# A decoder kernel on one Trainium2 core: the second composed weight by seven block products, with its sums of blocks on GpSimd, and the first weight weighed on ScalarE

## The chip, the cores and the metric

The kernel runs on one core of a Trainium2 chip. The metric is the device time of one execution in microseconds (us); lower is better. A core has five engines that run side by side and wait for each other by semaphores: TensorE (PE in the profile, its weight loads PEld) multiplies matrices into the accumulation memory PSUM, VectorE (DVE) and ScalarE (ACT) work elementwise and can read PSUM, GpSimd (POOL) works elementwise on SBUF only and issues the gathers here, and SyncE (SP) issues transfers.

## The reference, cut to what matters

The input x is 8 sequences of 256 tokens with 256 features, in float32. Three stages follow each other, each closed by x = layernorm(x + stage(x)):

1. four layers of self-attention (four local heads, four causal linear heads) and a two-layer perceptron of width 1024,
2. a cross-attention to a context,
3. a perceptron whose two weights are themselves composed:

```
vals, idx = top_k(logits, 32)
w = softmax(vals)
W = einsum('k,kir,kro->io', w, A[idx], B[idx])      # r = 64
# first weight:  A (64, 256, 64),  B (64, 64, 1024) -> W1 (256, 1024)
# second weight: A (64, 1024, 64), B (64, 64, 256)  -> W2 (1024, 256)
h = gelu(x @ W1);  y = h @ W2
```

The change is about composing W1 and W2. With the 32 chosen primitives stacked along r, each is a matrix product with an inner size of 32 x 64 = 2048. Neither depends on x, so the kernel composes them while the attention layers run.

## The kernel before

**Slots.** The main loop at line 1173 runs over slots s = 1 to 32 (four layers by eight sequences). In a slot several units at different stages interleave: `new` is the attention of unit s (projections, scores, exponentials), `old` that of unit s-1 (values and output projection), `after` that of unit s+1 (its moments, normalising and transposing), and `ff` the perceptron of unit s-4, which exists from s = 4 on. All engines but SyncE follow program order (`manual_schedule`, line 1101), so the order of calls in the loop is the order of each engine's queue. While the weights are being composed, `filled` is true (line 1177). A loop of 16 more slots from line 1283 does cross-attention and the composed perceptron.

**The composing.** It is split into 16 groups (line 321): eight for the first weight (n=0), eight for the second (n=1). A group has PG = 2 inner chunks of 128, that is two pairs of primitives. It passes four steps:

- `gather` (Group.__init__, line 325): GpSimd issues indirect transfers that fetch the rows of A (tiles `ga`) and of B (tiles `gbt`, of 128 x 1024 for n=0 and of 128 x 256 for n=1). It runs two groups ahead.
- `weigh` (line 341): A times its softmax weight, four VectorE instructions a group (L350), into `aw`.
- `turns` (line 359): TensorE transposes `aw` (L369) through PSUM banks, and VectorE and ScalarE copy the result to `at`. With at[k] as the stationary operand, this is A transposed, chunk k.
- `block` (line 382): four blocks of 128 x 512. For n=1 each block is two output rows j of 128 x 256, each accumulated over the two chunks k: 4 x 2 x 2 = 16 matmuls of 256 columns a group (L410). VectorE then copies the block to w2c (first group) or adds it to w2c (L420, L422). For n=0 w2c serves as the accumulator, and the last group writes w1c (L400).

`Compose.run` (line 448) does the blocks of the turned group, gathers one more group, and transposes the next. It is called three times in slot 1, twice in slots 2 and 3, and once, near the end of a slot, from slot 4 on. So the first weight is done in slot 4, and the second weight's eight groups are multiplied in slots 5 to 12. Before the loop, slot 0 (lines 1142 to 1167) weighs and transposes the first group.

**Seven products in the perceptron.** `Seven` (line 482) multiplies a matrix of two by two blocks with seven block products in place of eight (a scheme of Strassen's kind). Its products are `one` (line 509, L512: four matmuls of 128 columns each). The sums of blocks of the weights come once a layer from `first_sums` (L476 to L479), those of the tokens once a slot from `turn_sums` (L490 to L493), both on GpSimd.

**GpSimd's queue in a slot with `ff`.** In order: the power of `after.moments()` (L189), `ff.turn_sums()`, the memset of 64 columns of oT in `old.values()` (L801), two bias sums of `after.centre()` (L230), the power of `nxt_m.moments()`, the gathers of `compose.run()` (L302), two bias sums of `nxt_m.centre()`.

**TensorE's order in such a slot.** `new.qkv` (L602, L622), `old.linear_sums`, `old.turn_p` (L767), `ff.turn`, `new.scores` (L653), `old.values` (L784, L797), then `ff.p16` (products 1 and 6), `old.out(0)` (L240, which reads oT), `ff.p5`, `ff.p27`, `old.out(1)`, `ff.p34`, `ff.second(1)` (L561), `after.turn` (L213), `compose.run` (L410, L369), `ff.second(0)`.

**PSUM.** There are two pools of four banks each. Composing, `ff`, `turn` and `out` share `bank_g`; `second(1)` takes a bank there (ps_p_m) that `second(0)` fills up at the end of the slot.

Of the kernel before, what the change touches and what calls it, by code (L numbers as in the profile page):

```python
# [8 lines left out]
F32 = mybir.dt.float32  # L9
I32 = mybir.dt.int32  # L10
AF = mybir.ActivationFunctionType
ALU = mybir.AluOpType
# [3 lines left out]
P = 128  # L16
# [5 lines left out]
def tile_decoder_postln(  # L22
# [29 lines left out]
    nc = tc.nc  # L52

    B, T, D = x.shape
    DEPTH = Wq.shape[0]
    WT = T // P
    NC = D // P
    FF = W1.shape[2]
    NF = FF // P
    HL = 4  # L60
# [8 lines left out]
    NP, _, R = fc1_A.shape  # L69
    TOPK = 32  # L70
    NPAIR = TOPK // 2
# [30 lines left out]
    at = 0  # L102
    offs = {}
    for name, v in (("g1", ln1_g), ("b1", ln1_b), ("g2", ln2_g), ("b2", ln2_b), ("ff", b1)):
        n = v.shape[0] * v.shape[1] // P
# [17 lines left out]
    w1c = const.tile([P, NC, FF], F32, name="w1c")  # L123
    w2c = const.tile([P, NF, D], F32, name="w2c")
# [46 lines left out]
    def bank_g(name):  # L171
        return ps_g.tile([P, 512], F32, tag="bank_g", name=name)
# [78 lines left out]
    comp_stack = ExitStack()  # L251
    comp = comp_stack.enter_context(tc.tile_pool(name="comp", bufs=1))
# [59 lines left out]
    PG = 2  # L312
# [11 lines left out]
    class Group:  # L324
# [16 lines left out]
        def weigh(self):  # L341

            n, g, n_c = self.n, self.g, tables[self.n][2]
            wts = tops[n][2]
            self.aw = []
            for k, a in enumerate(self.a):
                t = g * PG + k
                aw = comp.tile([P, n_c, 2, R], F32, tag="aw", name=f"aw{n}_{t}", bufs=2)
                for e in range(2):
                    nc.vector.tensor_scalar(  # L350
                        aw[:, :, e, :],
                        a[:, e, :].rearrange("p (c r) -> p c r", c=n_c),
                        wts[:, 2 * t + e : 2 * t + e + 1],
                        None,
                        ALU.mult,
                    )
                self.aw.append(aw.rearrange("p c e r -> p c (e r)"))

        def turns(self):
            n, n_c = self.n, tables[self.n][2]  # L360
            self.at = []
            for k, aw in enumerate(self.aw):
                name = f"{n}_{self.g}_{k}"
                at_ = comp.tile([P, n_c * P], F32, tag="at", name=f"at{name}", bufs=4)
                for q in range(0, n_c, 4):
                    ps = bank_g(f"ps_at{name}_{q}")
                    m = min(4, n_c)
                    for c in range(m):
                        nc.tensor.transpose(ps[:, c * P : (c + 1) * P], aw[:, q + c, :], ident)  # L369
                    if n == 0:  # L370
                        copy = nc.scalar.copy if k else nc.vector.tensor_copy
                        copy(
                            at_.rearrange("q (p c) -> q c p", c=NC),
                            ps[:, : m * P].rearrange("q (c p) -> q c p", c=NC),
                        )
                    elif q == 0:
                        nc.vector.tensor_copy(at_[:, :512], ps)
                    else:
                        nc.scalar.copy(at_[:, 512:], ps)
                self.at.append(at_)  # L380

        def block(self, i):
            ps = bank_g(f"ps_w{self.n}_{self.g}_{i}")
            if self.n == 0:
                m, n = divmod(i, 2)
                for k in range(PG):
                    nc.tensor.matmul(  # L387
                        ps,
                        self.at[k][:, m * P : (m + 1) * P],
                        self.b[k][:, n * 512 : (n + 1) * 512],  # L390
                        start=k == 0,
                        stop=k == PG - 1,
                    )

                dst = w2c.rearrange("p f d -> p (f d)").rearrange("p (m o) -> p m o", m=NC)
                dst = dst[:, m, n * 512 : (n + 1) * 512]
                src = ps
                if self.g == NPAIR // PG - 1:
                    final = w1c[:, m, :].rearrange("q (j p) -> q p j", j=NF)
                    nc.vector.tensor_add(  # L400
                        final[:, n * 64 : (n + 1) * 64, :],
                        dst.rearrange("q (p j) -> q p j", j=NF),
                        src.rearrange("q (p j) -> q p j", j=NF),
                    )
                    return
            else:
                for e in range(2):
                    j = 2 * i + e
                    for k in range(PG):
                        nc.tensor.matmul(  # L410
                            ps[:, e * D : (e + 1) * D],
                            self.at[k][:, j * P : (j + 1) * P],
                            self.b[k],
                            start=k == 0,
                            stop=k == PG - 1,
                        )
                dst = w2c[:, 2 * i : 2 * i + 2, :].rearrange("p j d -> p (j d)")
                src = ps
            if self.g == 0:
                nc.vector.tensor_copy(dst, src)  # L420
            else:
                nc.vector.tensor_add(dst, dst, src)  # L422

    class Compose:

# [17 lines left out]
        def turn(self):  # L443
            self.turned, self.weighed = self.weighed, None
            if self.turned:
                self.turned.turns()

        def run(self):
            if self.turned is None:
                return  # L450
            if not self.weighed:
                self.weigh()
            for i in range(4):
                self.turned.block(i)
            self.gather()
            self.turn()

# [24 lines left out]
    class Seven:  # L482
# [26 lines left out]
        def one(self, n, ps, start=False, stop=False):  # L509

            for f in range(4):
                nc.tensor.matmul(  # L512
                    ps[:, f * P : (f + 1) * P],
                    self.ws[n][:, f * P : (f + 1) * P],
                    self.rhs[n],
                    start=start and f == 0,
                    stop=stop and f == 3,
                    skip_group_check=True,
                )
# [50 lines left out]
    class Attention:  # L570
# [99 lines left out]
        def exps(self):  # L670
            name = self.name
            nc.scalar.activation(self.qs, self.qs, AF.Exp)
            nc.scalar.activation(self.ke, self.ke, AF.Exp)
            self.p = []

            self.psum = small.tile([P, HL, 3], F32, tag="psum", name=f"psum_{name}")
            self.head_exps(range(2))

        def head_exps(self, heads):
            for h in heads:  # L680
# [211 lines left out]
    class Context:  # L892
# [29 lines left out]
        def take(self):  # L922
            b0, ps = self.b0, self.ps
            nc.vector.tensor_copy(
                self.cT[:, :, b0 : b0 + 2, :],
                ps[:, : 2 * NC * S2].rearrange("p (c b j) -> p c b j", c=NC, b=2),
            )
# [184 lines left out]
    compose = Compose()  # L1112
    cross = None
    cx = None
    new = Attention(0)
    first = {n: top_k(n) for n in range(2)}
# [43 lines left out]
    compose.gather()  # L1160
    new.scores()
    new.exps()
    new.head_exps((2, 3))
    new.softmax_q()
    new.totals()
    new.divide(range(HL))
# [1 line left out]
    old, new = new, after  # L1168
# [4 lines left out]
    for s in range(1, UNITS + 1):  # L1173
# [3 lines left out]
        filled = cross is None  # L1177
        if after and filled:
            after.moments()
        if new:  # L1180
            new.qkv(nxt_c)
        nxt_c = None
        if s == 1:
            compose.run()
        if s == 2:
# [5 lines left out]
        if ff:  # L1191
            ff.turn()
            ff.turn_sums()
        if new:
            new.scores()
        else:
            cx.sums()
# [35 lines left out]
        if turn_cx:  # L1233
            i = 2 * (s - (UNITS - B + LAG))
            cx.turn(i)
            cx.take()
        if new:
            new.exps()
        if ff:
            ff.second(1)  # L1240
        if after:
            after.turn()
        if new:
            new.head_exps((2, 3))
            new.softmax_q()
        if filled:
            compose.run()
# [6 lines left out]
            nxt_m.centre()  # L1254
        if ff:
            ff.second(0)
        if compose.done() and cross is None:
            comp_stack.close()
            cross = ctx.enter_context(tc.tile_pool(name="cross", bufs=1))
        l, b = divmod(s + 1, B)  # L1260
        if b == B - 2 and l + 1 < DEPTH:
            attn_ws[l + 1] = load_attn(l + 1, nc.scalar)
        l, b = divmod(s + 1 - LAG, B)
# [15 lines left out]
        old, new = new, after  # L1279
# [3 lines left out]
    for s in range(2 * B):  # L1283
        x, ff = nxt_x, nxt_m
        nxt_x = Cross(s + 1, cx) if s + 1 < B else None
        u = UNITS - LAG + s + 2
# [102 lines left out]
```

## Time and profile before

| | us |
|---|---|
| median of 3 runs (lowest to highest) | 1247.95 (1246.93 to 1251.23) |
| the profiled execution | 1256.8 |
| its span, first to last instruction | 1254.9 |
| TensorE busy | 1222.0 (97%) |
| weight loads busy (beside the matmuls) | 969.1 (77%) |
| VectorE busy | 847.8 (68%) |
| ScalarE busy | 628.7 (50%) |
| GpSimd busy | 382.7 (31%) |
| the second weight's matmuls, L410 | 56.6 (256 records) |
| the first weight's matmuls, L387 | 57.4 (128 records) |

Durations below come from the profiled execution. A line of a timeline reads: start, duration, engine, source line, operation, output <- inputs, and in brackets the idle time of the engine ahead of it and what ended it. A group of instructions reads: line, engine, operation, shapes and count, then busy time and mean ns of one, then idle time before. A float32 matmul leaves two records of matmul and two of weight load; matmuls overlap at their ends, so their pace is read from start to start. L12 is line 12 of the kernel.

### The profile page before, as it was taken

The page shows a single profiled execution, that of the slowest core. Times are in us where ns is not written, and L with a number is a line of the kernel's source. Part 1 is how long each engine was busy: PE and PEld are TensorE (multiplying, and loading weights), DVE is VectorE, ACT ScalarE, POOL GpSimd, SP SyncE. Part 2 cuts the span into 40 slices and gives each one's busy share as a digit, 9 for nine tenths or more (in the row PEclk, how much of TensorE's full clock was granted, in tenths as well). Part 3 has the DMA queues.
Part 4 walks back from the last instruction along what each step waited for, and adds up shares of the span by engine and source line. Part 5 has one row for each costly group of instructions (what it writes and reads, how often), then busy time and mean ns, then how long its engine had stood idle before and what let it go on. Part 6 is the DMA issues. An engine that isn't in the chain of part 4 may idle for free.

```text
span 1254.9 us, 23452 instructions
## 1 busy us (share of the span) xinstructions
PE 1222.0 (97%) x8905; PEld 969.1 (77%) x8905; DVE 847.8 (68%) x2435; ACT 628.7 (50%) x1738; POOL 382.7 (31%) x596
## 2 busy tenths in 40 slices
PE   5999999999999999999999999999999999999998
PEld 3555678888888888888878888788888777777787
DVE  5787877767767667777777776777765454556543
ACT  2222544555555556667766677566773334233322
POOL 5445433333334111222322221242213323222210
PEclk8998999999999999999999999999999999999999
DMA  4532212111120021002001000120000000000000
GB/s 131 168 91 83 81 51 81 43 43 43 65 73 20 1 84 39 2 2 72 1 1 39 2 1 17 57 69 1 26 10 10 9 9 9 18 17 9 9 14 22
DMA packets 29502, 47.77 MB, mean 38 GB/s; under 512 B 3150, under 2 KB 22734, under 8 KB 29134
## 3 DMA queue, kind: packets, MB, share of 16 engines
q0 software_dynamic: 6656, 20.98, 5.6%
q10 hardware_dynamic: 13024, 14.07, 3.4%
q1 hardware_dynamic: 9710, 11.23, 2.8%
q8 instruction: 70, 1.15, 0.4%
q14 instruction: 42, 0.34, 0.1%
HBM read 44.17 MB, written 2.10 MB: 37 GB/s over the span
## 4 chain that ended last, share of the span: by engine, by line
PE 92%; DVE 3%; ACT 2%; POOL 1%; issue 1%; another core or an unknown queue 0%; DMA 0%; POOLq 0%; ACTq 0%; DVEq 0%
PE ps_p_m L561 17%; PE qkv_a L622 8%; PE ps_h_m_u L512 7%; PE ps_h_m_a L512 5%; PE ps_w L387 4%; PE ps_w L410 4%; PE ps_h_m_d L512 4%; PE ps_p_a L240 4%; PE ps_qk_a L602 4%; PE ps_p_f L561 4%; PE ps_pT_a L767 3%; PE sc_a L653 3%; PE ps_y_c L1085 2%; PE ps_xq_c L996 2%; PE ps_xk_c L996 2%; PE ps_xv_c L996 2%
## 5 line engine op out<-in xcount | busy, mean ns | idle before, releaser
L561 PE MATMUL ps_p_m<-w,h_m 128*128 128x256 f32 x1024 | 231.5, 379 | 0.0
L561 PEld LDWEIGHTS ps_p_m<-w,h_m 128*128 128x128 f32 x1024 | 189.8, 190 | 23.5 <-ACT h_m L827 0.3
L622 PE MATMUL qkv_a<-wa,xT_a 128*128 128x512 f32 x256 | 115.7, 595 | 0.0
L230 POOL TENSOR_TENSOR x<-x,b 128x256 f32<-128x256 f32 x64 | 48.2, 773 | 209.5 <-DVE xn_m L195 209.4
L685 ACT ACTIVATE p_a<-sc_a,nm_a 128x128 f32<-128x128 f32 (+1 forms) x256 | 103.9, 426 | 1.9 <-DVE nm_a L666 1.7
L622 PEld LDWEIGHTS qkv_a<-wa,xT_a 128*128 128x128 f32 x256 | 49.1, 192 | 48.1 <-issue 46.3
L230 POOL TENSOR_TENSOR x<-x,bo 128x256 f32<-128x256 f32 x64 | 48.2, 772 | 118.4 <-DVE xn_a L195 113.6
L666 DVE TENSOR_REDUCE nm_a<-sc_a 128x1 f32<-128x128 f32 (+1 forms) x256 | 79.7, 353 | 4.4
L827 ACT ACTIVATE h_m<-h_m,cols 128x128 f32<-128x128 f32 x256 | 78.6, 405 | 6.2 <-DVE h_m L549 5.5
L512 PE MATMUL ps_h_m_a<-xT_m,w 128*128 128x128 f32 x512 | 71.4, 283 | 0.0
L302 POOL DMA_INDIRECT ga<-in_L_ffn_fc_A_dram,idx_a x64 | 62.1, 971 | 21.2 <-issue 16.6
L512 PE MATMUL ps_h_m_u<-tx_m,w 128*128 128x128 f32 x512 | 67.6, 275 | 0.0
L629 ACT COPY v<-qkv_a 128x256 f32<-128x256 f32 x64 | 23.8, 372 | 86.3 <-PE qkv_a L622 85.0
L602 PE MATMUL ps_qk_a<-xT_a,wa 128*128 128x256 f32 x256 | 64.0, 395 | 2.8 <-DVE nm_a L666 2.1
L512 PEld LDWEIGHTS ps_h_m_a<-xT_m,w 128*128 128x128 f32 x512 | 63.2, 194 | 4.2 <-issue 1.6
L240 PE MATMUL ps_p_a<-wo,oT_a 128*128 128x256 f32 x256 | 65.4, 380 | 0.0
L662 DVE TENSOR_TENSOR sc_a<-sc_a,causal 128x256 f32<-128x256 f32 x128 | 54.5, 425 | 15.5 <-PE sc_a L653 15.5
L715 DVE TENSOR_TENSOR p_a<-p_a,psum_a 128x384 f32<-128x384 f32 x128 | 62.9, 553 | 1.1
L512 PEld LDWEIGHTS ps_h_m_u<-tx_m,w 128*128 128x128 f32 x512 | 62.3, 192 | 0.0
L602 PEld LDWEIGHTS ps_qk_a<-xT_a,wa 128*128 128x128 f32 x256 | 50.4, 199 | 11.1 <-ACT p_a L685 2.8
L561 PE MATMUL ps_p_f<-w2c,h_f 128*128 128x256 f32 x256 | 57.8, 379 | 0.0
L767 PE MATMUL ps_pT_a<-ident,p_a 128*128 128x128 f32 x384 | 52.3, 278 | 5.6 <-ACT pT_a L772 5.0
(245 smaller groups left out, 2655.2 us busy)
## 6 DMA issues: line engine op xcount, KB each, us to landing
w<-in_L_attn_W_dram ACTq DMA_DIRECT2D x8, 1024.0 KB, 7.6
xwkv<-in_L_xattn_Wkv_dram SPq DMA_DIRECT2D x1, 2048.0 KB
x_c<-in_x_dram SPq DMA_DIRECT2D x8, 256.0 KB, 2.7
out_dram<-y_f SPq DMA_DIRECT2D x16, 128.0 KB, 1.7
x<-in_x_dram ACTq DMA_DIRECT2D x6, 256.0 KB, 2.7
ga<-in_L_ffn_fc_A_dram,idx_a POOLq DMA_INDIRECT x64
xwq<-in_L_xattn_Wq_dram SPq DMA_DIRECT2D x1, 1024.0 KB
xwo<-in_L_xattn_Wout_dram SPq DMA_DIRECT2D x1, 1024.0 KB
```

What stands on the lines that cost most here:

```text
L230: nc.gpsimd.tensor_add(xb[:, i, :], xb[:, i, :], bias)
L240: nc.tensor.matmul(ps[:, i * D : (i + 1) * D], lhs(c, i), w[:, c, :], start=c == 0, stop=c == n_in - 1,)
L512: nc.tensor.matmul(ps[:, f * P : (f + 1) * P], self.ws[n][:, f * P : (f + 1) * P], self.rhs[n], start=start and f == 0, stop=stop and f == ...
L561: nc.tensor.matmul(self.ps[:, i * D : (i + 1) * D], self.h[k][:, f, :], self.w2[:, half * 4 + f, :], start=k in (11, 22) and f == 0, stop= ...
L602: nc.tensor.matmul(ps[:, s * T : (s + 1) * T], wa[:, c, s * HW : (s + 1) * HW], xT[:, c, :], start=c == 0, stop=c == NC - 1,)
L622: nc.tensor.matmul(t, xT[:, c, w * P : (w + 1) * P], wa[:, c, 2 * HW :], start=c == 0, stop=c == NC - 1,)
L666: nc.vector.tensor_reduce(self.nmax[:, h, w : w + 1], sc[:, s], AX.X, ALU.max, negate=True)
L685: nc.scalar.activation(flat[:, s], sc[:, s], AF.Exp, bias=self.nmax[:, h, w : w + 1], accum_out=self.psum[:, h, w : w + 1],)
L715: nc.vector.tensor_tensor(p, p, self.psum[:, h, :, None].to_broadcast([P, 3, P]), ALU.mult)
L767: nc.tensor.transpose(pp[:, k * P : (k + 1) * P], p[:, k, :], ident)
L827: nc.scalar.activation(dst[:, f, :], src[:, f * P : (f + 1) * P], AF.Gelu, bias=col("ff", i))
L996: nc.tensor.matmul(ps[:S2], lhs(c), w[:, c, off : off + 512], start=c == 0, stop=c == NC - 1)
```

## The change

- **Second weight by seven products.** `block` keeps only the first weight's case. For n=1, `seven` computes the group's product, a matrix of 2 x 2 blocks (each 512 x 128, inner size 128) by seven block products of four matmuls of 128 columns: 28 matmuls a group. They accumulate in banks p6, p12, p53 and p74; VectorE takes from these in seven instructions of 128 x 512, into the four quarters of w2c and into `u`, a common sum that all groups share.
- **Sums of blocks.** `combine(0)`, called after `new.qkv` at the top of the next slot, forms four sums of 128 x 128 of B and two of 128 x 512 of A on GpSimd; `combine(1)`, called after `ff.turn_sums`, two more of 128 x 512 of A. Two of the eight are written in place.
- **`final`** adds `u` to three quarters of w2c: three GpSimd sums of 128 x 512, at the top of slot 13. The composing pool is closed there, not at the end of slot 12, and so slot 13 still counts as `filled`.
- **First weight weighed on ScalarE**: `weigh` for n=0 issues `nc.scalar.mul`; for n=1 it stays on VectorE.
- **Exponentials.** `exps` no longer calls `head_exps(range(2))`. In filled slots all four heads' exponentials follow `after.turn()`; in others two come before `ff.second(1)`, as they did.
- **`at`** has two buffers instead of four.

The diff, cut to its core:

```diff
@@ weigh
-                    nc.vector.tensor_scalar(
-                        aw[:, :, e, :],
...
+                    if n == 0:
+                        nc.scalar.mul(dst, src, w)
+                    else:
+                        nc.vector.tensor_scalar(dst, src, w, None, ALU.mult)
@@ turns
-                at_ = comp.tile([P, n_c * P], F32, tag="at", name=f"at{name}", bufs=4)
+                at_ = comp.tile([P, n_c * P], F32, tag="at", name=f"at{name}", bufs=2)
@@ block
-            else:
-                for e in range(2):
-                    j = 2 * i + e
-                    for k in range(PG):
-                        nc.tensor.matmul(
-                            ps[:, e * D : (e + 1) * D],
-                            self.at[k][:, j * P : (j + 1) * P],
-                            self.b[k],
...
+        def combine(self, part):
+            if part:
+                a, s2, s4 = self.rest
+                nc.gpsimd.tensor_sub(s4, a[0][1], s2)
+                nc.gpsimd.tensor_sub(a[1][0], a[0][0], a[1][0])
+                return
+            a = [[at_[:, m * 512 : (m + 1) * 512] for at_ in self.at] for m in range(2)]
+            b = [[b_[:, n * P : (n + 1) * P] for n in range(2)] for b_ in self.b]
...
+            nc.gpsimd.tensor_sub(t1, b[0][1], b[0][0])
+            nc.gpsimd.tensor_sub(t2, b[1][1], t1)
+            nc.gpsimd.tensor_sub(t4, b[1][0], t2)
+            nc.gpsimd.tensor_sub(b[0][1], b[1][1], b[0][1])
+            nc.gpsimd.tensor_add(s1, a[1][0], a[1][1])
+            nc.gpsimd.tensor_sub(s2, s1, a[0][0])
...
+        def one(self, i, ps, start=False, stop=False):
+            a, b = self.factors[i]
+            for f in range(4):
+                nc.tensor.matmul(
+                    ps[:, f * P : (f + 1) * P],
+                    a[:, f * P : (f + 1) * P],
+                    b,
...
+        def seven(self):
...
+            def take(dst, ps, first=False):
+                src = ps.rearrange("p (f i) -> p f i", f=4)
+                if self.g == 0 and first:
+                    nc.vector.tensor_copy(dst, src)
+                else:
+                    nc.vector.tensor_add(dst, dst, src)
...
+            self.one(6, p6, True, True)
+            take(u, p6, True)
...
+            self.one(1, p12, start=True)
+            take(u, p12)
...
+            self.one(5, p53, start=True)
+            take(c[1][1], p53, True)
...
+            self.one(7, p74, start=True)
+            take(c[1][1], p74)
+            self.one(2, p12, stop=True)
+            take(c[0][0], p12, True)
+            self.one(3, p53, stop=True)
+            take(c[0][1], p53, True)
+            self.one(4, p74, stop=True)
+            take(c[1][0], p74, True)
...
+        def final(self):
+            for m, n in ((0, 1), (1, 0), (1, 1)):
+                c = w2c[:, 4 * m : 4 * m + 4, n * P : (n + 1) * P]
+                nc.gpsimd.tensor_add(c, c, Group.u)
@@ the loop over slots
         if new:
             new.qkv(nxt_c)
         nxt_c = None
+        if filled:
+            compose.combine(0)
+            if compose.done():
+                compose.last.final()
+                comp_stack.close()
+                cross = ctx.enter_context(tc.tile_pool(name="cross", bufs=1))
...
         if ff:
             ff.turn()
             ff.turn_sums()
+            compose.combine(1)
...
         if new:
             new.exps()
+            if not filled:
+                new.head_exps((0, 1))
...
         if after:
             after.turn()
         if new:
-            new.head_exps((2, 3))
+            new.head_exps((2, 3) if not filled else range(HL))
```

## The prediction

> **What bounds the kernel now.** I read four views of the run before: the chain that ended last, busy time by stretches, then the timelines of TensorE, GpSimd, VectorE and ScalarE in one slot of the changed kind and at the start. The chain:
>
> ```profile
> PE 92%; DVE 3%; ACT 2%; POOL 1%; issue 1%; another core or an unknown queue 0%; DMA 0%; POOLq 0%; ACTq 0%; DVEq 0%
> ```
>
> TensorE is the path almost throughout. Stretches (us; busy and count of PE, PEld, DVE, ACT, POOL; granted clock, DMA share, GB/s):
>
> ```profile
> 0.00:32.00 32.00, 17.83 (x58) 11.31 (x59) 17.77 (x67) 8.92 (x29) 17.88 (x34) 0.84 0.44 136
> 60.00:100.00 40.00, 36.94 (x204) 21.09 (x203) 32.80 (x92) 12.89 (x51) 21.02 (x23) 1.00 0.35 105
> 309.00:344.00 35.00, 35.00 (x272) 29.27 (x272) 25.06 (x69) 18.38 (x52) 12.49 (x18) 1.00 0.15 50
> ```
>
> From 180 to 480 us TensorE never idles (the list of its waits is empty there), and the eight groups of the second weight lie there, in slots s=5 to 12. So in these slots each TensorE microsecond saved or stalled is one of the total. Before 180 us it has gaps.
>
> **Edit 1: 16 products of 256 columns become 28 of 128.** A float matmul leaves two records. TensorE's timeline in slot s=9 (start, us, count):
>
> ```profile
> 319.31 1.16 PE L512 MATMUL ps_h_m_a<-xT_m,w 128*128 128x128 f32 x8
> 320.30 1.06 PE L512 MATMUL ps_h_m_u<-tx_m,s 128*128 128x128 f32 x8
> 321.19 1.03 PE L240 MATMUL ps_p_a<-wo,oT_a 128*128 128x256 f32 x4
> 322.06 1.05 PE L512 MATMUL ps_h_m_d<-tx_m,s 128*128 128x128 f32 x8
> ...
> 331.28 7.07 PE L410 MATMUL ps_w<-gbt,at 128*128 128x256 f32 x32
> 338.19 2.20 PE L369 MATMUL ps_at<-ident,aw 128*128 128x128 f32 x16
> ```
>
> From start to start, the old group takes 338.19 - 331.28 = 6.91 us. One block product of the same shape as the new ones (L512, eight records) takes 321.19 - 320.30 = 0.89 us, so seven take 6.23. Gain 0.68 a slot, 5.4 over eight. The Trainium skill speaks against it here (TensorE: Matmul & The Clock Gate, "Back-to-back issue gap"): a sustained stream of weight loads and matmuls is spaced 81 ns at 128 columns and 131 ns at 512, so narrow matmuls pay for their weight load. By a straight line between these (an estimate from that page, about 98 ns at 256) 28 narrow ones would cost 1.45 times 16 wide ones, a loss of 3.1 us a slot. In float the rows decide otherwise: 216 ns a record wide (6.91/32), 111 ns narrow (0.89/8), a ratio of 1.94. I take the rows.
>
> **Its seven reads of PSUM.** VectorE now has 7 adds of 128x512 for 4. Its timeline in the old block (idle in brackets):
>
> ```profile
> 333.31 0.68 DVE L422 TENSOR_TENSOR w2c<-w2c,ps_w 128x512 f32<-128x512 f32 x1
> 334.94 0.69 DVE L422 TENSOR_TENSOR w2c<-w2c,ps_w 128x512 f32<-128x512 f32 x1 [0.95 <-PE ps_w L410]
> ```
>
> Three gaps of about 1 us take the three more (3 x 0.6, their spacing back to back). But VectorE is free only at 333.31, 2.03 after TensorE begins, and ps_p_m keeps one of four banks for second(0) at the slot's end. So p74 takes p6's bank, free at 333.31 + 0.68 + 0.1 = 334.1, while TensorE wants it at 331.28 + 3 x 0.89 = 333.95: stall 0.15. The later products find their adds done (product 2 wants its bank at 335.0, free at 334.8; 4 at 336.8, free at 336.2). Bounds: 0 with a fourth bank; 0.5 if an add of four runs of 128 took L400's 1.04 us; I take 0.15, since the read with inner runs of 120 (L1075, 648 ns for 480) keeps the plain rate. After product 4 one add follows, as before.
>
> **Edit 2: the sums on GpSimd.** Its timeline in the same slot, and from its groups the rate of a 128x512 sum:
>
> ```profile
> 311.09 0.72 POOL L189 TENSOR_TENSOR rs_a<-rs_a,neghalf 128x2 f32<-128x2 f32 x1 [1.03 <-DVE rs_a L184]
> 317.75 0.45 POOL L490 TENSOR_TENSOR tx_m<-xT_m 128x128 f32<-128x128 f32 x1 [5.93 <-DVE xT_m L222]
> ...
> 319.23 0.45 POOL L493 TENSOR_TENSOR tx_m<-xT_m,tx_m 128x128 f32<-128x128 f32 x1
> 319.63 0.15 POOL L801 MEMSET oT_a<- 128x64 f32 x1
> ...
> L476 POOL TENSOR_TENSOR s<-w 128x512 f32<-128x512 f32 x4 | 5.1, 1273 | 0.0
> ```
>
> Part 0 follows the power at 311.8: four sums of 128x128 (0.41, or 0.5 where one needs the last: 1.8) and two of 128x512 (1.3 each) end near 316.3. The next work, turn_sums, can't begin before 317.75: hidden with 1.4 to spare. Part 1 stands behind turn_sums and **ahead of the memset of values()**: two sums, 2.5 us, so the memset goes from 319.63 to about 322.1 and ends at 322.25. The one who waits is out(0), the L240 line at 321.19. Its first matmul reads the other half of oT; the second, at 321.19 + 0.43 = 321.62, reads the columns that the memset fills. It resumes near 322.35 (0.1 from release to matmul: aw ended at 23.26 and ps_at began at 23.37). **Stall 0.73 us a slot**, all of TensorE queued behind. Bounds 0.5 (sums overlapping at their ends) and 1.0 (1.35 us each, as L477 to L479). The shifted memset delays nothing else on GpSimd: the bias sums wait for xn_a until 323.02.
>
> The Trainium skill (SBUF — State Buffer, "SBUF: two separate sides") names a lock that would make it worse: a VectorE instruction with two SBUF inputs can't run beside a GpSimd one that reads SBUF. In the window of part 0 that is only cn_a (L757, 316.42), just after its end; in that of part 1 none. I take 0.05 a slot, bounds 0 and 0.3.
>
> **Edit 3: weighing of the first weight on ScalarE.** 32 instructions (453 ns mean) leave VectorE, where four of these eight groups took 1.8 to 3.4 us beside GpSimd sums for 0.9 to 1.1 otherwise. In slots 1 to 3 no TensorE wait is on aw or on VectorE's lateness that this would cure, so gain 0. At the start it is on the path:
>
> ```profile
> 22.87 0.56 ACT L223 ACTIVATE xT_a<-ps_t_a,cols 128x256 f32<-128x256 f32 x1 [5.20 <-DVE xT_a L222]
> 22.75 1.01 DVE L350 TENSOR_SCALAR aw<-ga,wts 128x128 f32<-128x128 f32 x4
> 23.37 1.13 PE L369 MATMUL ps_at<-ident,aw 128*128 128x128 f32 x4 [1.12 <-DVE aw L350]
> ```
>
> VectorE weighed while ScalarE did its half of xT_a. Now four ScalarE instructions (0.3 apart, 0.4 long, as L827's rows from SBUF) begin at 23.33; the last ends at 24.65, ps_at ends at 25.3 for 24.43, and the scores, whose maxima on VectorE hold qk at 28.2, follow: +0.85. All heads' exponentials now stand after xT_a: in the last run of slot 3, ScalarE waits for xT_a until 127.8, exponentiates to 131.55, and weighs to 132.85, where ps_at wants it at 132.67: +0.3. In slots 1 and 2 the same ends 0.7 us or more ahead. Sum +1.15, bounds 0 and 1.6.
>
> **What costs nothing.** Two at tiles for four: the copies follow transposes that stand behind the matmuls which read the old ones. xT_a's ScalarE half ahead of the exponentials: its bank is free at 332.5 where p53 wants it at 333.06. final() in slot 13: three sums, 3.9 us, after the power, ahead of turn_sums with the margin of part 0. Slot 13 keeps the filled order once more: nothing seen to pay.
>
> **Sum.** Eight slots: 8 x (-0.68 + 0.15 + 0.73 + 0.05) = +2.0; start +1.15; **+3.2 us**. The profiled execution took 1256.8 (span 1254.9, 1.9 around it) and would take 1260.0; the median of three is 1247.95, so **1251.2**.
>
> **Rivals.**
> 1. *The memset doesn't hold out(0)* (the sums finish sooner, or the matmul runs ahead). Then 8 x (-0.68 + 0.15) + 1.15 = -3.1: 1244.9. For: 0.73 is a small difference of modelled ends. Against: program order on GpSimd, and 2.5 us of sums for 1.6 to 2.0 of slack. 0.17.
> 2. *Slower by far: TensorE's instructions arrive late.* At the start this is seen: in the stretch 100 to 112, one 16 KB instruction packet travels among gathers, everyone waits for 3.54 us in the chain ("another core or an unknown queue"), and then TensorE runs slow:
>
> ```profile
> q8 instruction: 1, 0.02, 0.8%
> ...
> 110.01 0.90 PE L767 MATMUL ps_pT_a<-ident,p_a 128*128 128x128 f32 x3 [2.98 <-ACT pT_a L772]
> 110.84 2.35 PE L653 MATMUL sc_a<-qk_a 32*128 32x128 f32 x16
> ```
>
> L653 takes 1.32 in later slots. With L784, L797 and L387 slow too, some 2.7 us more: about 6 in all. The change adds 24 records of matmuls and as many loads in each of eight slots, so fetches fall elsewhere. Against: a fetch in 196 to 206 amid gathers stalled nothing. It decides from one new stall on: 1251.2 + 5.7 = 1256.9. 0.15.
> 3. *VectorE sets the pace*: adds at L400's 1.04: 8 x 0.45 more, 1254.8. 0.08.
> 4. *The start gains*: lighter VectorE lets one of the gaps before 180 us go, some 6 us and less: 1245 or below. 0.07.
>
> **How the numbers follow.** The forecast itself (1248 to 1253.5) has 0.53. A change within 0.3% (3.7 us) can't be told from none by a measurement of this kernel. Slower by more (over 1251.7): 0.20 of the forecast's share, rivals 2 and 3: 0.43. Faster (under 1244.2): a third of rival 1 and most of 4: 0.11. Same 0.46. Range 1244.5 (rival 1) to 1257 (rival 2).
>
> **What would show it.** Seven products in about 6.4 us from first to next transpose; an idle of 0.7 ahead of L240's second matmul in slots 5 to 12, its releaser GpSimd's memset; ps_at at 24.2 at the start. Wrong if TensorE has no wait in those slots (rival 1), or one of over 1.5 us (rival 2).

## The result, and the profile after

| | before | after |
|---|---|---|
| median of 22 runs each (lowest to highest), us | 1249.92 (1246.93 to 1253.08) | 1253.78 (1252.84 to 1256.88) |
| the profiled execution, us | 1256.8 | 1253.36 |
| its span, us | 1254.9 | 1251.4 |
| from the first qk of slot 5 to that of slot 13, us | 276.75 | 280.82 |

The change made the kernel slower: the ratio of the times is 1.0035, with an interval of 1.0026 to 1.0044, and the two medians differ by 3.86 us. (The profiled execution of before lies above all of its timed runs, and so the two spans say nothing of the change; the last row does.) The kernel before took 1249.7 to 1258.8 us from one session to another, so every kernel below is compared with the runs of before that were made beside it.

The page of the changed kernel has less TensorE in the chain that ended last, and a group that waits for GpSimd:

```profile
PE 87%; DVE 6%; POOL 3%; ACT 3%; issue 1%; DMA 0%; POOLq 0%; ACTq 0%; DVEq 0%
...
L240 PE MATMUL ps_p_a<-wo,oT_a 128*128 128x256 f32 x256 | 67.5, 383 | 3.6 <-POOL oT_a L882 3.6
```

The same stretch as before, one slot long (busy and count of PE, PEld, DVE, ACT, POOL; clock, DMA share, GB/s): TensorE, which was busy for 35.00 of 35.00 us, now idles for 0.45, and GpSimd has 18.60 for 12.49:

```profile
309.00:344.00 35.00, 34.55 (x294) 29.17 (x293) 26.70 (x71) 18.28 (x52) 18.60 (x25) 1.00 0.33 102
```

TensorE's waits between 161 and 445 us, that is in slots 5 to 12, where the list was empty before (us in total, times, longest):

```profile
PE ps_p_a L240 <- POOL oT_a L882: 3.6, 8, 0.5
PE ps_w L449 <- DVE csum_u L468: 0.5, 1, 0.5
```

These waits are 4.1 us in all, and the products save time on top; so they can't be the whole of +4.07. What else there is shows only in the timeline. A slot that was 34.85 us from qk to qk is 35.28 now. TensorE in slot s=9 of the changed kernel:

```profile
310.53 1.51 PE L735 MATMUL sc_a<-qk_a 32*128 32x128 f32 x16
311.97 0.86 PE L865 MATMUL ps_ao_a<-pT_a,v 128*32 128x128 f32 x24
...
315.12 0.60 PE L240 MATMUL ps_p_a<-wo,oT_a 128*128 128x256 f32 x2
316.17 0.70 PE L240 MATMUL ps_p_a<-wo,oT_a 128*128 128x256 f32 x2 [0.45 <-POOL oT_a L882]
316.70 1.05 PE L594 MATMUL ps_h_m_d<-tx_m,s 128*128 128x128 f32 x8
...
325.93 1.06 PE L449 MATMUL ps_w<-ct_pb,cs 128*128 128x128 f32 x8
...
332.36 2.20 PE L369 MATMUL ps_at<-ident,aw 128*128 128x128 f32 x16
```

Before, the scores and the small VectorE addition `rk_a` in the same slot were:

```profile
316.00 0.17 DVE L754 TENSOR_SCALAR rk_a<-cs_a 128x3 f32<-128x3 f32 x1
316.80 1.32 PE L653 MATMUL sc_a<-qk_a 32*128 32x128 f32 x16
318.05 0.86 PE L784 MATMUL ps_ao_a<-pT_a,v 128*32 128x128 f32 x24
```

Read from start to start, three stretches differ from before: the products take 332.36 - 325.93 = 6.43 for 6.91 (-0.48); out(0) takes 316.70 - 315.12 = 1.58 for 0.87 (+0.71); and the scores take 311.97 - 310.53 = 1.44 for 1.25 (+0.19), without a wait that the list would show. The sum is +0.42. GpSimd and VectorE in the slot of the changed kernel say why:

```profile
308.80 1.28 POOL L434 TENSOR_TENSOR cs<-cs,at 128x512 f32<-128x512 f32 x1
309.74 0.36 DVE L835 TENSOR_SCALAR rk_a<-cs_a 128x3 f32<-128x3 f32 x1
310.52 0.55 DVE L851 COPY pT_a<-ps_pT_a 128x384 f32<-128x384 f32 x1
313.50 1.29 POOL L417 TENSOR_TENSOR cs<-at,cs 128x512 f32<-128x512 f32 x1
314.76 1.27 POOL L418 TENSOR_TENSOR at<-at 128x512 f32<-128x512 f32 x1
315.96 0.15 POOL L882 MEMSET oT_a<- 128x64 f32 x1
```

The memset ends at 316.11, and out(0) resumes at 316.17. And rk_a, 0.17 us long before, lasts until GpSimd's second sum ends at 310.08. Behind it in VectorE's queue stands the copy of pT_a, which frees a PSUM bank that the scores of one head need: these 0.19 us are TensorE's.

Slot 11 has 0.6 us more than that (35.88). There `first_sums` of the next layer runs, once, beside the seven products, and the reads come late:

```profile
397.58 1.34 POOL L559 TENSOR_TENSOR s<-s,w 128x512 f32<-128x512 f32 x1
398.39 0.82 DVE L781 TENSOR_TENSOR qs_a<-qs_a,qsum_a 128x256 f32<-128x256 f32 x1
399.13 1.47 DVE L468 TENSOR_TENSOR csum_u<-csum_u,ps_w 128x512 f32<-128x512 f32 x2
399.86 2.05 PE L449 MATMUL ps_w<-gbt,at 128*128 128x128 f32 x16 [0.51 <-DVE csum_u L468]
```

L781 took 0.43 in slot 9. Before, the same instruction was held in slot 11 too, and there it cost nothing, since VectorE sat idle for about 1 us between two reads of the old products:

```profile
402.95 0.81 DVE L700 TENSOR_TENSOR qs_a<-qs_a,qsum_a 128x256 f32<-128x256 f32 x1
```

So slots 5 to 12 have 7 x 0.43 + 1.03 = +4.04 us, within 0.03 of the measured +4.07.

### The profile page after: what moved, and what is told of

The parts are those of the page before. It is cut to its first block, busy times and chain, and to the rows that moved or that the text cites. A ratio compares the mean times of both kernels' runs of the same rounds, so it can differ in the third digit from the quotient of the medians.

```text
span 1251.4 us, 23979 instructions
## 1 busy us (share of the span) xinstructions
PE 1219.8 (97%) x9097; PEld 970.4 (78%) x9097; DVE 853.4 (68%) x2427; ACT 640.1 (51%) x1770; POOL 438.4 (35%) x663
## 3 DMA queue, kind: packets, MB, share of 16 engines
q8 instruction: 72, 1.18, 0.4%
## 4 chain that ended last, share of the span: by engine, by line
PE 87%; DVE 6%; POOL 3%; ACT 3%; issue 1%; DMA 0%; POOLq 0%; ACTq 0%; DVEq 0%
PE ps_p_m L643 17%; PE qkv_a L704 8%; PE ps_h_m_u L594 6%; PE ps_w L387 4%; PE ps_h_m_d L594 4%; PE ps_h_m_a L594 4%; PE ps_p_a L240 4%; PE ps_qk_a L684 4%; PE ps_w L449 4%; PE ps_p_f L643 4%; PE sc_a L735 2%; PE ps_pT_a L848 2%; PE ps_y_c L1166 2%; PE ps_xq_c L1077 2%; PE ps_xk_c L1077 2%; PE ps_xv_c L1077 2%
## 5 line engine op out<-in xcount | busy, mean ns | idle before, releaser
L704 PE MATMUL qkv_a<-wa,xT_a 128*128 128x512 f32 x256 | 116.7, 599 | 0.0
L704 PEld LDWEIGHTS qkv_a<-wa,xT_a 128*128 128x128 f32 x256 | 49.7, 194 | 48.7 <-issue 46.8
L744 DVE TENSOR_TENSOR sc_a<-sc_a,causal 128x256 f32<-128x256 f32 x128 | 54.5, 425 | 14.6 <-PE sc_a L735 14.6
L387 PE MATMUL ps_w<-gbt,at 128*128 128x512 f32 x128 | 56.6, 595 | 0.0
```

Source lines behind the costliest of these rows:

```text
L387: nc.tensor.matmul(ps, self.at[k][:, m * P : (m + 1) * P], self.b[k][:, n * 512 : (n + 1) * 512], start=k == 0, stop=k == PG - 1,)
L704: nc.tensor.matmul(t, xT[:, c, w * P : (w + 1) * P], wa[:, c, 2 * HW :], start=c == 0, stop=c == NC - 1,)
```

## The experiments

Theory: the products gain as forecast, and the sums cost by their place in GpSimd's queue. They do it through the memset behind them, and through a port of SBUF that they hold while VectorE needs it ("the lock" below). Rivals: the time lies at the start; or the sums' 7 us a slot on GpSimd cost by their amount, wherever they stand. Four kernels ran in each of three sessions. "Slots" below are slots 5 to 10, qk to qk.

### The memset ahead of the second pair of sums

```diff
             ff.turn_sums()
-            compose.combine(1)
...
         old.values()
+        if ff:
+            compose.combine(1)
```

> The two late sums of blocks stand behind the memset of values() instead of ahead of it; nothing else differs from the changed kernel. If out(0) waits for the memset (0.71 us a slot from start to start in the trace of the changed kernel), eight slots give back 5.7 us: about 1248.1 us, no wait on the memset, a slot of 34.6 us for 35.3. If the seven products and their reads of PSUM are the cost, or the weighing on ScalarE, it stays near 1253.8.

1265.47 us for 1258.78 of before, ratio 1.0048 (1.0031 to 1.0065): a miss. The wait on the memset is gone, and slot 5 takes 34.63 us, but every later one about 35.6. In such a slot (VectorE, GpSimd, TensorE):

```profile
251.31 0.43 DVE L835 TENSOR_SCALAR rk_a<-cs_a 128x3 f32<-128x3 f32 x1
251.79 1.26 POOL L434 TENSOR_TENSOR cs<-cs,at 128x512 f32<-128x512 f32 x1
251.98 1.19 DVE L838 TENSOR_TENSOR cn_a<-cs_a,rk_a 128x96 f32<-128x96 f32 x1
253.10 0.55 DVE L851 COPY pT_a<-ps_pT_a 128x384 f32<-128x384 f32 x1
253.70 0.92 PE L735 MATMUL sc_a<-qk_a 32*128 32x128 f32 x10 [0.91 <-DVE pT_a L851]
```

cn_a, 0.26 us long elsewhere, ends when the sum does, and the scores wait for 0.91. The sum begins 7.65 us after the slot, not 6.23 as in the changed kernel, because VectorE came to the slot late and GpSimd's power waits for VectorE. So the same lock costs 0.2 us or 1.2 by where the sum falls.

### The first weight weighed on VectorE again

```diff
-                    if n == 0:
-                        nc.scalar.mul(dst, src, w)
-                    else:
-                        nc.vector.tensor_scalar(dst, src, w, None, ALU.mult)
+                    nc.vector.tensor_scalar(dst, src, w, None, ALU.mult)
```

> The changed kernel with the first weight weighed on VectorE again. If the weighing on ScalarE costs only at the start (ps_at 0.75 us later, the first blocks of the first weight 2.06 us later at 37.08 for 35.02), this gains 2 us: 1251.7, with the slots 5 to 12 as in the changed kernel (35.3 us). If that weighing were the whole loss, it comes to 1250 or below. If it also spares the waits for instructions of the first slots, those come back and it gains nothing: 1252 to 1256.

1267.94 us, ratio 1.0066 (1.005 to 1.0082). The start is regained (the qk of slot 1 at 28.09 for 29.09). But four of its slots take about 36.26 us, with cn_a at 1.18 as above, and two take 35.28. Nothing in the edit touches those slots; VectorE was late in the four, and they met the lock in its worse place. In slots 5 to 12 this kernel differs from the first experiment by the place of the second pair alone, ahead of the memset here and behind it there, and the two ran in one session: 35.28 against 34.63 where VectorE is in time, and 36.26 against 35.6 where it is late. So moving the pair is worth 0.65 us in both kinds of slot.

### The kernel before, once more

> The kernel before once more, for a second trace. If its waits for instructions in the first slots (in the first trace about 2.5 us at 44 to 48, 3 to 6 us at 105 to 115, 1.5 us at 140) vary from execution to execution, its span differs from 1254.9 by some us while slots 5 to 12 keep 34.85 us each. If they belong to the kernel, they stand at the same places with the same sizes.

One run, 1260.8 us. Its slots are 34.85 to the digit, so that length is the kernel's own. Slot 5 begins at 171.73 us, 2.3 later than in the first trace of the same kernel (169.44). That it begins at 161.43 in the changed kernel's trace can therefore not be put down to the change.

### No sums at all

```diff
         def combine(self, part):
...
-            nc.gpsimd.tensor_sub(t1, b[0][1], b[0][0])
...
-            nc.gpsimd.tensor_sub(s2, s1, a[0][0])
+            s1, s2, s4 = a[1][0], a[0][0], a[0][1]
+            t1, t2, t4 = b[0][1], b[1][1], b[1][0]
```

This kernel leaves out all eight sums of blocks, so its second weight is not the reference's; products, reads and `final` stay.

> The changed kernel with the eight sums of blocks left out: the seven products take blocks as they are, so the second weight is not the reference's. Matmuls, reads of PSUM and the final sums stay. If the sums on GpSimd cost 0.71 (memset) and 0.19 (VectorE held by the port at the reciprocal's scalar add) a slot, this is 7.2 us faster than the changed kernel, 1246.6, with a slot of 34.4 us. If the products or their reads cost, it stays near 1253.8.

1255.84 us, ratio 0.9977 (0.9969 to 0.9985): faster than before. Slots take 34.38 (-0.47). TensorE from the products to the transposes:

```profile
331.12 6.59 PE L435 MATMUL ps_w<-gbt,at 128*128 128x128 f32 x56
337.55 2.20 PE L369 MATMUL ps_at<-ident,aw 128*128 128x128 f32 x16
```

6.43 us, as with the sums. So the seven products and reads gain what the trace of after showed, and all that is lost in these slots is the sums'. (Slot 11 still takes 0.6 more, 34.96: its wait comes from `first_sums`, not from the sums left out.)

### The changed kernel again

> The changed kernel itself, unaltered, beside the three others of this call. If the shared port is what made two of the first four experiments' slots long, the length of a slot depends on when VectorE starts it: slots 5 to 12 take 35.28 us where VectorE's first instructions of the slot are in time (as in the changed kernel's first profile), and about 36.2 us where they are 1.4 us late and cn_a (L838) falls behind GpSimd's second sum. If instead the 35.28 belongs to this kernel by its own order of work, all eight slots take 35.28 again. Ratio to the kernel before: 1.0035 in the first case of the first profile, up to 1.006 with long slots.

1253.95 us for 1249.66, ratio 1.0035 (1.002 to 1.005). Slots of 35.28 us, all with rk_a at 0.36 to 0.38: +4.02 us from slot 5 to 13.

### All four large sums behind the centring

```diff
             if part:
+                nc.gpsimd.tensor_add(s1, a[1][0], a[1][1])
+                nc.gpsimd.tensor_sub(s2, s1, a[0][0])
                 nc.gpsimd.tensor_sub(s4, a[0][1], s2)
...
-            compose.combine(1)
...
+            compose.combine(1)
             old.out(0)
```

> The changed kernel with its four sums of 128x512 issued behind old.values() and after.centre(), ahead of old.out(0), instead of two at the top of the slot and two ahead of the memset of oT_a; ScalarE still weighs the first weight. Theory: the sums cost only through the memset that waits behind them (0.71 us a slot) and through the port they hold while VectorE's rk_a and cn_a are due (0.19, or about 1.2 in the long slots); both go, and slots 5 to 12 take 34.4 us as in the kernel without sums (34.38), so 8 x 0.9 = 7 us less than the changed kernel and some 4 less than before with a start that is 2 us late: ratio to before 0.998. The weighing of the next pair (L356, four of 0.42 us) may be held by the sums beside it, up to 1.7 us, but TensorE doesn't need it for another 9 us. Rival: GpSimd's 7 us of added work delays whatever comes behind it (x plus bias L230, power L189, the gathers), wherever it stands: slots of 35.0 us or more, and a ratio of 1.001 or more.

1252.42 us, ratio 1.0029 (1.002 to 1.0038); slots of 35.10. These are the rival's numbers, and a miss of the theory by 0.7 a slot; but the rival's reason, the amount of the sums, is not what the trace shows. The expectation named the weighing as held and thought it free. Memset and rk_a cost nothing here. But:

```profile
319.18 1.29 POOL L419 TENSOR_TENSOR cs<-at,cs 128x512 f32<-128x512 f32 x1
319.29 3.66 DVE L356 TENSOR_SCALAR aw<-ga,wts 128x512 f32<-128x512 f32 x4
320.43 1.45 POOL L420 TENSOR_TENSOR at<-at 128x512 f32<-128x512 f32 x1
325.96 1.48 DVE L468 TENSOR_TENSOR csum_u<-csum_u,ps_w 128x512 f32<-128x512 f32 x2
326.79 2.02 PE L449 MATMUL ps_w<-gbt,at 128*128 128x128 f32 x16 [0.29 <-DVE csum_u L468]
```

The weighing takes 3.66 us for 1.67, VectorE begins the reads of the products 2.69 us after the first product (323.27) instead of 2.02, and the products need 7.16 us for 6.43: all of the 0.7 that was missing. The same kernel with the weighing on VectorE:

> As the kernel with the sums behind, and with the first weight weighed on VectorE as before. Theory: the weighing on ScalarE alone puts the start back by 0.9 us at the first qk and 2.1 us at the first product of the composition (37.08 for 35.02), so this kernel is 2 us below the other one with late sums, some 6 us below the kernel before, ratio 0.9955. Rival: the waits for instructions in slots 0 to 4 take up a late start, so that the two kernels with late sums agree within 0.5 us.

1251.52 us, ratio 1.0015 (1.0006 to 1.0024), with slots of 35.10 too: 0.9 us less by the medians for the start, between what theory and rival said. The two intervals overlap, so this pair alone doesn't show the difference.

### One part alone: the kernel before, first weight on ScalarE

> The kernel before with one part of the change alone: the first weight's weighing on ScalarE (head_exps stays where it was). Theory: the start costs 0.9 us at the first qk, 2.1 us at the first product of the composition and 0.2 us at the fourth slot, so 2 to 2.3 us more than before, ratio 1.0018. Rival: the waits for instructions in slots 0 to 4 absorb it: within 0.5 us of before.

1250.03 us for 1249.66, ratio 0.9999 (0.9986 to 1.0011): no difference that can be told, as the rival said, though ps_at waits for 1.82 us (1.12 before) and the first product of the composition comes at 35.99 for 35.02.

### The sums in two pairs, each where VectorE reads PSUM

s1 and s2 go behind `old.values()`, s4 and the last sum behind `after.centre()`; the four small ones stay at the top of the slot. The first weight is weighed on VectorE.

```diff
         old.values()
+        if ff:
+            compose.combine(1)
...
+            compose.combine(2)
             old.out(0)
```

> The changed kernel with the first weight weighed on VectorE, and the four sums of 128x512 in two pairs: s1 and s2 behind old.values() (behind the memset of oT_a, where VectorE works on scores in PSUM), s4 and the seventh product's sum behind after.centre() (ended before VectorE weighs at L356). Theory: each cost of the sums is a place, not their time: the memset no longer waits, rk_a and cn_a aren't held, and the weighing, held from 1.67 to 3.66 us in the kernel with all four sums behind the centring, is free again, so the seven products don't wait for their reads. Slots 5 to 12 take 34.4 us (34.38 without sums), 8 x 0.47 = 3.8 us less than before: ratio to before 0.997, the first version under both kernels. Rival: the sums always hold some VectorE instruction that TensorE needs (x plus projection L234 or xn_a L195 here), and slots stay at 34.85 or more, ratio 1.000 or more.

1254.32 us for 1257.16, **ratio 0.9975 (0.9967 to 0.9983): below the kernel before**, and with slots of 34.43 for 35.28 below the changed kernel. VectorE and GpSimd in one slot:

```profile
314.69 0.17 DVE L835 TENSOR_SCALAR rk_a<-cs_a 128x3 f32<-128x3 f32 x1
318.25 0.15 POOL L882 MEMSET oT_a<- 128x64 f32 x1
318.36 1.28 POOL L414 TENSOR_TENSOR cs<-at,at 128x512 f32<-128x512 f32 x1
318.62 0.42 DVE L744 TENSOR_TENSOR sc_a<-sc_a,causal 128x256 f32<-128x256 f32 x1
324.42 1.27 POOL L420 TENSOR_TENSOR at<-at 128x512 f32<-128x512 f32 x1
325.98 1.67 DVE L353 TENSOR_SCALAR aw<-ga,wts 128x512 f32<-128x512 f32 x4
```

All sums are there, as long as ever, and cost nearly nothing (34.43 for the 34.38 without sums): rk_a has its 0.17, the mask on the scores in PSUM (L744) its 0.42 beside a sum, and the weighing its 1.67 behind the last one. This holds in the slots to which VectorE comes late, too (slot 8 by 1.7 us, 34.43). So the amount of the sums, the second rival, is out. With the first weight on ScalarE:

> The same, with the first weight weighed on ScalarE as in the changed kernel. Theory: the weighing on ScalarE costs 0.7 us at the first transposes, and with the clock that rises later 1 to 2 us by the first composed product; lowest time of this kernel above the other's by 0.8 to 1.8 us, as between the two kernels with late sums (1251.44 and 1249.62). Rival: no difference beyond 0.4 us, as the medians of the kernel before with and without it say (1250.03 and 1249.66).

1257.17 us, ratio 0.9997 (0.9989 to 1.0006): the same slots (34.43), 2.85 us more.

### One sum moved from the top of the slot

s2 moves from the top of the slot to the pair ahead of the memset, and the last sum behind `old.values()`.

> The changed kernel with one of its sums, s2 (128x512), and s4 that needs it, in other places: s2 opens the pair that stands ahead of the memset, and the seventh product's sum goes behind old.values(). So the top of the slot holds one sum, and the memset still waits behind two. Theory: the port lock on rk_a (0.36 for 0.17, and the scores 0.19 us late) goes, the stall at the memset stays at 0.7 us: slots 5 to 12 take 35.28 - 0.19 = 35.1 us. Rival: the late scores have another cause (VectorE's order of work at the top of the slot), and the slots stay at 35.28.

1264.39 us, ratio 1.0057 (1.0043 to 1.0071); slots stay near 35.3: a miss. In slots 5, 7, 8 and 9, rk_a has its 0.17 and the scores their 1.25, so the lock was their cause. In slots 6 and 10 VectorE is late, the one sum that is left falls beside rk_a, and rk_a takes 0.30 to 0.32 and the scores 1.38 to 1.40. And everywhere the wait at the memset grew:

```profile
321.73 1.28 POOL L417 TENSOR_TENSOR cs<-cs,at 128x512 f32<-128x512 f32 x1
323.09 1.29 POOL L418 TENSOR_TENSOR cs<-at,cs 128x512 f32<-128x512 f32 x1
324.32 0.14 POOL L885 MEMSET oT_a<- 128x64 f32 x1
324.52 0.70 PE L240 MATMUL ps_p_a<-wo,oT_a 128*128 128x256 f32 x2 [0.58 <-POOL oT_a L885]
```

The second sum of the pair now needs the first, and the pair takes 2.59 us to the memset for 2.46 (+0.13). The products take 6.50 for 6.43, as in every kernel here with sums directly behind `old.values()`; why is open. What the top of the slot gave, these two took.

### The first experiment once more

> The kernel of the first experiment (second pair of sums behind old.values(), so behind the memset), once more, on a chip on which the changed kernel's slots take 35.28 us if it is like the last one. Theory: the memset is worth 0.71 us a slot and the port lock at the top of the slot 0.19 as long as VectorE starts the slot in time: slots of 34.56 us, ratio 0.9995. Rival: the 35.6 us of the first experiment belong to the kernel (its sums push VectorE late into the next slot's top by themselves), and come again.

1260.77 us, ratio 1.0024 (1.0014 to 1.0035). Neither theory alone: good and bad slots alternate in one trace, and VectorE's place decides. Worked out from its timelines (the starts in us from the slot's qk; under rk_a and cn_a how long each took):

| slot | xn_m (L195) starts | s2 (L434) starts | rk_a | cn_a | length of slot |
|---|---|---|---|---|---|
| 5 | -0.82 | 6.22 | 0.36 | 0.26 | 34.63 |
| 6 | -0.54 | 6.23 | 0.37 | 0.26 | 34.63 |
| 8 | +0.12 | 6.78 | 0.93 | 0.26 | 35.19 |
| 7 | +0.92 | 7.60 | 0.37 | 1.19 | 35.57 |

The good slots are 0.65 below 35.28: out(0) has its 0.87 again (-0.71), and the products take 6.50 (+0.07). The others are the lock, and it grows with VectorE's lateness.

The lateness itself is not made by the sums. In the kernel without sums xn_m starts at +0.93 to +0.96 in slots 6 to 10, as late as in the worst slots here, and the slots keep their 34.38: late VectorE costs only where a sum then holds the port. Nor did the kernel before show it in its second trace, in the same session (-0.83 to -0.91). All late slots stand in traces of the two sessions in which before took 1257 to 1259 us; the changed kernel was traced only in the others. What makes VectorE late is open: its second copy of the transposes (L377) is released 0.66 us later in the slot before slot 8 than in the slot before slot 9, though TensorE's records of the transposes look alike.

### All runs together

The difference of a kernel's median to before's, split by its trace into slots 5 to 12 (276.75 us before) and the rest. Where good and late slots mix (memset first, VectorE weighs, one sum late), they can differ from run to run, and the split is rough: the same kernel has +4.79 in one trace and +2.14 in the other.

| kernel | first weight on | median | slots 5 to 12 | rest |
|---|---|---|---|---|
| changed | ScalarE | +3.86 | +4.07 | -0.21 |
| changed, again | ScalarE | +4.29 | +4.02 | +0.27 |
| four sums behind | ScalarE | +2.76 | +1.83 | +0.93 |
| before, ScalarE weighs | ScalarE | +0.37 | -0.03 | +0.40 |
| memset first | ScalarE | +6.69 | +4.79 | +1.90 |
| no sums | ScalarE | -2.94 | -3.22 | +0.28 |
| sums split | ScalarE | +0.01 | -2.74 | +2.75 |
| one sum late | ScalarE | +7.23 | +4.38 | +2.85 |
| memset first, again | ScalarE | +3.61 | +2.14 | +1.47 |
| VectorE weighs | VectorE | +9.16 | +8.95 | +0.21 |
| four sums behind | VectorE | +1.86 | +1.87 | -0.01 |
| sums split | VectorE | -2.84 | -2.72 | -0.12 |

With VectorE weighing, the slots account for the whole difference within 0.2 us. With ScalarE weighing there is a rest of -0.2 to 0.9 where before took 1249.7 to 1249.9 us (the first four), and of 0.3 to 2.9 where it took 1257 to 1259. One pair shows the late start cleanly, "sums split" with and without it (2.85 us, intervals apart); in the sessions of the result something took it up. What took it up is open. Slot 5 begins at 160.4 to 164.5 us in the five traces that belong to a before of 1249.7 to 1249.9 us, and at 169.5 to 173.9 in the eight of the two other sessions, before's second trace among them: it goes with the session more than with the kernel. (Before's first trace, at 169.4, was slower than all its timed runs.)

## Why the prediction was right, and where it wasn't

The forecast was 1251.2 us, +3.2 on the median it started from; measured were 1253.78 and +3.86. That is inside the range of 1244.5 to 1257, and just above the 1248 to 1253.5 of the forecast itself, since before's median over 22 runs is 1249.92, not 1247.95. That +3.86 comes so near to +3.2 is luck, two errors of opposite sign: slots 5 to 12 cost 4.07 us for 2.0, and the start next to nothing for 1.15. Of the 2.07 us that the slots cost more, the lock is 1.1 (8 x 0.14), slot 11 is 0.6, and the products' smaller gain 0.4. Nor is 0.3% the least that can be told from none, as the prediction held: the interval of "sums split", at 0.9975, leaves out 1.

- **Seven products** (-0.68 + 0.15 = -0.53 a slot): -0.48. The rows decided rightly: the float records keep 111 ns at 128 columns, and the 1.45-fold cost that the spacing on the Trainium skill's page (TensorE: Matmul & The Clock Gate, "Back-to-back issue gap") would give does not appear.
- **The memset behind the sums** (+0.73 a slot): +0.71 from start to start, and the experiment that moved it gave back these 0.71. Rival 1 is out.
- **The port lock** (0.05 a slot, bounds 0 and 0.3): **the step that failed**. It was 0.19 in every slot, inside the bounds, and 0.75 to 1.2 in the other kernels where the sum fell 0.6 to 1.4 us later. The prediction said that in part 0's window "that is only cn_a", just after its end. For cn_a it took one trace's margin of a tenth of a microsecond for safety. And it missed rk_a, a small tensor_scalar on VectorE that reads SBUF alone: by the prediction's own times it starts at 316.00, inside a window that ends near 316.3. It had given half of the rule. The Trainium skill (SBUF — State Buffer, "SBUF: two separate sides") names an exclusive lock for the whole instruction, on the VectorE side not only for an instruction with two SBUF inputs but also for one in a mode that uses both of its ports. cn_a (1.19 us for 0.26) has two inputs. rk_a, xn_a and the weighing have one tensor and were held as well; that they ran in such a mode no trace here says. The kernel before showed it already, and the prediction read it: the weighing took "1.8 to 3.4 us beside GpSimd sums", here beside `first_sums`, for 0.9 to 1.1 otherwise.

```profile
94.78 3.35 DVE L350 TENSOR_SCALAR aw<-ga,wts 128x128 f32<-128x128 f32 x4
95.15 1.28 POOL L476 TENSOR_TENSOR s<-w 128x512 f32<-128x512 f32 x1
```

- **Eight equal slots**: slot 11 was another 0.6, since `first_sums` holds VectorE ahead of the seven reads there. The sum named no GpSimd work other than the change's own.
- **The start** (+1.15): ps_at at 24.12 for 23.37 and qk 0.89 later, as said. In the changed kernel's trace, the first product of the composition is even 2.06 later (37.08 for 35.02), since the clock rises later (granted 0.84 for 1.00 from 33 to 38 us): L704 takes 4.57 us for 3.60. But of this the timed runs of the result keep nothing that can be told. Slot 3's +0.3 was 0.18 (the last transposes take 0.61 up to qk, for 0.43).
- **Rival 2** (late instructions): no such wait in slots 5 to 12. **Rival 3** (adds at 1.04): the reads take 0.7 each. **Rival 4**: the start gained nothing. What was put at nothing nearly was: slot 13, with `final` at its top, keeps its 25.90 us, and slot 14 has 0.21 more.

## What to carry to other kernels

Work handed to an idle engine cost here by what stood behind it in that engine's queue and by what it held up on another, not by its own time: the same 7 us of sums a slot cost 0.9 us in one place and 0.05 in another. Before placing a GpSimd operation, list for its whole window, with a margin of 1 to 2 us on either side (VectorE's lateness changed by up to 1.8 us from slot to slot here), each VectorE instruction that works on SBUF alone, and what TensorE waits for behind it; put the GpSimd work where VectorE reads PSUM. And where a small release (here a memset of 0.15 us) stands at the end of a queue, issue it ahead of the bulk work.

## What the runs showed that was not expected

- The lock weighs on the smallest instructions as on large ones: the weighing, one tensor from SBUF and a scalar a partition, took 3.66 us for 1.67, xn_a (L195) 1.50 for 0.73, and rk_a, 128x3, up to 0.93 for 0.17. The mask on the scores, which reads PSUM, kept 0.42.
- With the lock, a slot's length depends on how late VectorE comes to it: 34.63, 35.19 and 35.57 us in one trace of one kernel, with the same instructions. Without sums, or with the sums beside reads of PSUM, VectorE was as late and the slots stayed equal.
- A wait that was always there became a cost when the work behind it grew denser: `first_sums` held VectorE before the change as well (0.81 us), and only the seven reads made TensorE wait for it.
- A start that is 0.89 us late at qk was 2.06 us late at the first composed product, the granted clock being 0.84 for 1.00 between 33 and 38 us.
